# Last three head groups by halves, own buffers for the last batch, and four reorderings, in a fused adaLN attention and adapter block

## The chip, the cores and the metric

One Trainium2 chip, one core, one launch. The metric is the device time of the kernel in microseconds (us). The kernel before took 1140.43 us, the median of three runs (1139.66 to 1143.99).

## The reference

For each of 4 sequences of 1024 tokens and 256 channels (float32): a modulated layer norm, attention with 16 heads of 16 channels, a gated residual, a second modulated norm, and a feed-forward part that picks one of 8 adapters per sequence by the smallest reconstruction loss.

```python
mod = (silu(c) @ wmod).reshape(4, 6, 1, 256)          # sa, ca, ga, sb, cb, gb; |ga|, |gb| at least 0.25
h = layernorm(x) * (1 + ca) + sa
q, k, v = split(h @ qkv_w.T)                          # 16 heads of 16
x = x + ga * (softmax(q @ k.T * 0.25) @ v @ proj_w.T + proj_b)
h = layernorm(x) * (1 + cb) + sb
recon = relu(h @ W_enc[n] + b_enc[n]) @ W_dec[n] + b_dec[n]     # for all 8 n
top = argmin_n mean((recon - h) ** 2)                 # one n per sequence
ad = connected_idx[top]
out = x + gb * (h @ W_base + b_base + relu(h @ W_down[ad] + b_down[ad]) @ W_up[ad] + b_up[ad])
```

## The kernel before

**Steps.** The heads go in groups of 4, so there are 16 groups (b, g), four for each batch b. The scores of a group are made transposed, keys on the partitions, for one half h of the queries (512) and one tile of 128 keys at a time. That is a step: `begin` twice (four matmuls each into `pt`, L707, then an exponential on ACT, L715, into `es`) and `weigh` once (eight matmuls `pv`, L664). A half (b, g, h) has 8 steps, so the list `order` of 32 halves has 256 steps, and the main loop takes two steps at a time (an iteration, k0 = 0, 2, 4 ...). In the order before, both halves of a group stand next to each other, except at the end, where the first halves of groups (3,2) and (3,3) come before their second ones.

**Row maxima.** The exponent needs the maximum of each query's row before the step. `row_max` makes the scores a second time, queries on the partitions, in 32 "pairs" for each group (16 for each half): two matmuls `ps` (L604) and a max on DVE (L611). After the 16 pairs of a half, `to_row` is put in the list `urgent`: a transpose `pmx` on PE (L564), copies on DVE and POOL (L566 to L570), then `store`, which writes the maxima to DRAM (L573), and `back`, which reads them as rows into the tile `mt` (two transfers, L584). The second matmul pair of each `pt` (`pt<-mt,pick`) subtracts them, so the first step of a half needs `mt`. How many pairs stand done at step k is said by `wanted(k)`, a straight line between the points of the list `ends`.

**The planner.** `defer(n, f)` runs f at the n-th `tick` from now; there is one tick at the start of each step. Everything else is in streams: lists of items that wait for a step ("at"), for so many steps ("wait"), or for a condition ("need"), and then emit moves ("X"), dense matmul tiles ("D") or decode tiles ("R"). An iteration has a fixed pattern of tiles, score pairs and weighings (`PATTERN`). At its first V an urgent `to_row` is taken if there is one; otherwise one D, if the streams are pressed, that is if the sum of their paces is over 1.2. At its end it takes one D if one was ready at its top. Up to two R go in an iteration. A stream with a due step (`by`) gets a pace and a rate from what is left; R is taken twice in an iteration only if some stream's rate is over 1. PE and SP run in exactly the order in which they are emitted; the other engines are reordered from step 16 on.

**q and k.** `expand` brings a group's q and k back from DRAM, 256 KB in each of eight transfers (L525), into tiles of three buffers; `fetches` does so from step n * 16 + 1 on for the group n + 2, once the q and k of its channel half are stored.

**After attention.** `post(b)` projects the attention's output of a half (`ppj`, L757), adds the residual, norms (bn_stats, POOL's power, transposes `ptn_n`), encodes (`ph`, L793; ACT, L801) and decodes (`pr`, L814; DVE subtracts, L817; ACT squares and sums, L822). When both halves are done, `choose` (L836 to L868) finds the adapter and gathers its weights, `narrow` makes `pmid` (L905), and `final` makes the last product (`pf`, L928 and L939), added on DVE (L948). `post(b)` runs beside the steps of batch b + 1. For the last batch, the streams called `ending` start with group (3,3), but the first item of `main` waits for the end of post(2), since both use the same buffers (x, gates, gated weights, h2T). What is left of `ending` after the steps goes in an order written out by hand in the last lines.

**The divisor.** For the last channel half of the last batch the sums of the exponentials come straight from `ou` to `su` (L683), and `scaled_last(h)` takes the reciprocal (L650) and multiplies (L651), in two pieces of 256 columns one after the other; the projection of that half needs it.

Of the kernel before, what the change touches and what calls it, by code (L numbers as in the profile page):

```python
# [17 lines left out]
P = 128  # L18
HD = 16
HG = 4  # L20
# [6 lines left out]
def tile_adaln_block(  # L27
# [257 lines left out]
    def defer(steps, f):  # L285
        later.append([steps, f])
# [270 lines left out]
    def row_max(b, g):  # L557

        n = (b * NG + g) % 2
        mx = st.tile([P, NH, NH, HG, TH], F32, tag="mx", name=f"mx_{b}_{g}", bufs=2)  # L560

        def to_row(hq):
            pm = msc_tile([P, P], f"pmx_{b}_{g}_{hq}")
            nc.tensor.transpose(pm, mpad[n], ident)  # L564
            mfull = st.tile([HG * NT, P], F32, tag="mfull", name=f"mfull_{b}_{g}", bufs=1)
            nc.vector.tensor_copy(mfull, pm[: HG * NT, :])  # L566
            mrow = st.tile([HG * NT, 2, P], F32R, tag="mrow", name=f"mrow_{b}_{g}", bufs=1)
            eng = nc.vector if alone else nc.gpsimd
            eng.tensor_copy(mrow[:, 0, :], mfull)  # L569
            eng.tensor_tensor(mrow[:, 1, :], mfull, mrow[:, 0, :].bitcast(F32), ALU.subtract)  # L570

            def store():
                nc.sync.dma_start(  # L573
                    mdram[n][hq].rearrange("l r c -> r l c"),
                    mrow[hq * HG * TH : (hq + 1) * HG * TH].bitcast(F32),
                )
                if alone:
                    back()
                else:
                    defer(1, back)  # L580

            def back():
                for a in range(2):
                    nc.sync.dma_start(  # L584
                        mt[n][a * DUO : a * DUO + HG, hq * HALF : (hq + 1) * HALF].bitcast(F32),
                        mdram[n][hq, :, a * HG * TH // 2 : (a + 1) * HG * TH // 2, :].rearrange(
                            "l (i t) c -> l i (t c)", i=HG // 2
                        ),
                    )

            if alone:
                store()
            else:
                defer(1, store)

        for half in range(NH):
            pairs = [(i, half, t, h) for h in range(NH) for i in range(2) for t in range(TH)]
            for i, hq, t, h in pairs:
                q, k = duos["q", b, g, i], duos["k", b, g, i]
                t0 = hq * HALF + t * P  # L600
                ps = big_tile([P, 2, HALF], f"ps_{b}_{g}_{hq}_{t}_{h}_{i}")
                for a in range(2):
                    r = slice(a * DUO, (a + 1) * DUO)
                    nc.tensor.matmul(  # L604
                        ps[:, a, :],
                        q[r, t0 : t0 + P],
                        k[r, h * HALF : (h + 1) * HALF],
                        start=True,
                        stop=True,
                    )  # L610
                nc.vector.tensor_reduce(mx[:, h, hq, i::2, t], ps, AX.X, ALU.max, negate=True)  # L611
                if (i, hq, t, h) == pairs[-1]:
                    rows = mpad[n][:, : HG * NT].rearrange("p (q j t) -> p q j t", q=NH, t=TH)
                    nc.vector.tensor_tensor(rows[:, half], mx[:, 0, half], mx[:, 1, half], ALU.min)
                    defer(1, lambda half=half: urgent.append(("D", 0.0, [lambda: to_row(half)])))
                yield
# [26 lines left out]

    last_su = {}

    def scaled_last(h):
        su, part = last_su[h], aT_of[B - 1, h][:, NC - 1, :]
        for u in range(2):
            cols = slice(u * HALF // 2, (u + 1) * HALF // 2)
            nc.vector.reciprocal(su[:, cols], su[:, cols])  # L650
            nc.vector.tensor_tensor(part[:, cols], part[:, cols], su[:, cols], ALU.mult)  # L651

    def step_of(b, g):
# [6 lines left out]
        def weigh(h, kt, es):  # L660
# [10 lines left out]
            if kt == NT - 1:  # L671
                if (b, h) not in aT_of:
                    aT_of[b, h] = wp.tile([P, NC, HALF], F32, tag="aT", name=f"aT_{b}_{h}", bufs=3)
                ou = wp.tile([P, HALF], F32, tag="ou", name=f"ou_{b}_{g}_{h}", bufs=1)
                nc.scalar.copy(ou, acc[h])
                to = slice(r0, r0 + HG * HD)
                at = aT_of[b, h][to, ch, :]
                if (b, ch) == (B - 1, NC - 1):
                    nc.sync.dma_start(at, ou[0::2, :])
                if (b, ch) == (B - 1, NC - 1):  # L680
                    if h not in last_su:
                        last_su[h] = wp.tile([P, HALF], F32, tag="su", name=f"su_{b}_{ch}_{h}", bufs=1)
                    nc.sync.dma_start(last_su[h][to, :], ou[1::2, :])  # L683
                    if g == NG - 1 and h < NH - 1:
                        defer(2, lambda: scaled_last(h))
                        defer(4, lambda: done.add((b, ch, h)))
                    return
                j0 = (g % GC) * HG

                def keep():  # L690
                    nc.sync.dma_start(at, ou[0::2, :])
                    nc.sync.dma_start(sdram[ch * NH + h][j0 : j0 + HG, :], ou[1::STRIP, :])
                    if g % GC == GC - 1:
                        defer(1, lambda: turned(b, ch, h))
                        defer(8, lambda: done.add((b, ch, h)))

                defer(1, keep)
# [23 lines left out]
    def post(b, last=False):  # L721
# [1 line left out]
        s = {}  # L723

        def load():
            s["x"] = wp.tile([P, NT, D], F32, tag="x", name=f"x_{b}", bufs=1)
            src = x[b].rearrange("(t p) d -> p t d", p=P)
            for h in range(NH):
                nc.sync.dma_start(
                    s["x"][:, h * TH : (h + 1) * TH, :], src[:, h * TH : (h + 1) * TH, :]  # L730
                )
            s["gt"] = wp.tile([P, 2, D], F32, tag="gt", name=f"gt_{b}", bufs=1)

            nc.gpsimd.dma_start(s["gt"], gates[b].partition_broadcast(P))

# [3 lines left out]
        def gate_proj():  # L739

            ga = s["gt"][:, 0, :]
            s["wpg"] = wp.tile([P, NC, D], F32, tag="wg", name=f"wpg_{b}", bufs=1)
            nc.gpsimd.tensor_tensor(s["wpg"], wproj, per_chunk(ga), ALU.mult)
            s["gpb"] = wp.tile([P, D], F32, tag="gxb", name=f"gpb_{b}", bufs=1)
            nc.gpsimd.tensor_tensor(s["gpb"], ga, pb, ALU.mult)

        def biased(u, what):
# [18 lines left out]
                nc.vector.tensor_tensor(xs, s["po"], xs, ALU.add)  # L766

        def alloc():
            s["h2T"] = wp.tile([P, NC, S], F32, tag="h2T", name=f"h2T_{b}", bufs=1)
            s["acc"] = st.tile([P, NE, NC, NH], F32, tag="sq", name=f"acc_{b}", bufs=1)  # L770

        def normed(half):
            return norm_items(
# [188 lines left out]
        def rec(pr, h):  # L962
            return [("R", lambda c=c: decode(pr, c, h)) for c in range(NC)]

        main = [("need", (b - 1, "end")), ("wait", 2), ("X", load), ("X", alloc), ("wait", 1), ("X", gate_proj)]
        main += [("X", lambda u=u: biased(u, "gpb")) for u in range(NT // 2)]
        for h in range(NH):
            main += [("need", (b, ch, h)) for ch in range(NC)]
# [9 lines left out]
        recs.append(("done", (b, "r")))  # L978
        tail = [("need", (b, "r")), ("wait", 3), ("D", 0.1, [choose]), ("X", gate_out)]
        tail += [("X", lambda u=u: biased(u, "gbb")) for u in range(NT // 2)]  # L980
        tail += [("wait", 1), ("D", FULL, [lambda c=c: narrow(c) for c in range(NC)]), ("wait", 1)]
        each = [(u, t) for u in range(NT // 2) for t in range(2)]
        if last:
            first = [v for v in each if early(v[0])]
# [19 lines left out]

    X_AT = {1: (0, 2), 2: (STEPS + 4, STEPS + 10), 3: (3 * STEPS + 8, 3 * STEPS + 14)}

    groups = [(b, g) for b in range(B) for g in range(NG)]

    order = [(b, g, h) for b, g in groups for h in range(NH)]
    order[-3], order[-2] = order[-2], order[-3]  # L1010
    first_step = {}
    for n, (b, g, h) in enumerate(order):
        first_step.setdefault((b, g), n * NT)
# [152 lines left out]

    def all_maxima():
        yield from maxima
        for b, g in groups[1:-2]:
            yield from row_max(b, g)  # L1170
        last = [row_max(*bg) for bg in groups[-2:]]
        for n in range(2 * PAIRS):
            yield next(last[n * NH // PAIRS % 2])

    def wanted(k):

        ends = [(0, FIRST + 3), (NT - LEAD, PAIRS), (len(order) * NT - NT - LEAD, len(groups) * PAIRS)]
        for (k0, n0), (k1, n1) in zip(ends, ends[1:]):
            if k < k1:
                return n0 + (n1 - n0) * (k + 1 - k0) // (k1 - k0)  # L1180
# [4 lines left out]
    def fetches():  # L1185

        moves = []
        for n, (b, g) in enumerate(groups[2:]):
            moves += [("at", n * STEPS + 1)] + [("need", (w, b, g // GC)) for w in "qk"]
            moves += [("X", lambda b=b, g=g, i=i: expand(b, g, i)) for i in range(2)]  # L1190
            if n + 2 >= NV:
                moves += [("need", ("v", b, NT // 2 - 1)), ("X", lambda b=b, g=g: fetch_v(b, g))]
# [88 lines left out]
    for k0 in range(0, len(order) * NT, 2):  # L1281
        b, g, h = order[k0 // NT]
        if k0 == first_step[b, g]:
# [6 lines left out]
                    left = [36, 28, 28, 18, 12, 0] if b < B - 1 else [34, 26, 26, 12, 8, 0]  # L1290
                    streams += [Stream(items, end - n) for items, n in zip(post(b - 1), left)]
            if (b, g) == groups[-1]:
                ending = [Stream(items) for items in post(B - 1, last=True)]
                streams += ending[:-2]
        if k0 == STEPS:
            begin_order.close()
# [99 lines left out]
```

## Time and profile before

| what | value |
|---|---|
| median of three runs | 1140.43 us |
| the profiled execution | 1141.97 us, span 1140.1 us |
| PE busy | 1079.2 us (95%) |
| DVE busy | 797.2 us (70%) |
| ACT busy | 702.6 us (62%) |
| POOL busy | 262.3 us (23%) |
| last weighing ends, span ends | 1073.1 us, 1140.1 us |
| granted clock of PE, mean | 0.984 |

The times below are of the profiled execution, counted from the start of its span. The activations of L715 are 512, two for each step, so counting them dates each step: step 16 begins its first one at 129.7, step 224 at 953.0, step 240 at 1010.4 and step 246 at 1047.0 us. A number in square brackets at the end of a timeline row is the idle time of that engine just before, and what ended it.

### The profile page before, as it was taken

The page shows a single profiled execution, that of the slowest core. Times are in us where ns is not written, and L with a number is a line of the kernel's source. Part 1 is how long each engine was busy: PE and PEld are TensorE (multiplying, and loading weights), DVE is VectorE, ACT ScalarE, POOL GpSimd, SP SyncE. Part 2 cuts the span into 40 slices and gives each one's busy share as a digit, 9 for nine tenths or more (in the row PEclk, how much of TensorE's full clock was granted, in tenths as well). Part 3 has the DMA queues.
Part 4 walks back from the last instruction along what each step waited for, and adds up shares of the span by engine and source line. Part 5 has one row for each costly group of instructions (what it writes and reads, how often), then busy time and mean ns, then how long its engine had stood idle before and what let it go on. Part 6 is the DMA issues. An engine that isn't in the chain of part 4 may idle for free. (4 is left out here: it accounts for less than half of the span.)

```text
span 1140.1 us, 16544 instructions
## 1 busy us (share of the span) xinstructions
PE 1079.2 (95%) x6371; PEld 482.7 (42%) x6371; DVE 797.2 (70%) x958; ACT 702.6 (62%) x953; POOL 262.3 (23%) x309
## 2 busy tenths in 40 slices
PE   8989899999999999999999999999998999999995
PEld 3433334443444444444544443333544334334433
DVE  5687677667767676777678777877688777872373
ACT  3246566666556677776455777776465677754672
POOL 2214234213243121112435100003221000041103
PEclk9899999999999999999999999999999999999997
DMA  6522423232340302123150303021140200002001
GB/s 185 103 66 90 153 78 119 85 118 71 130 153 39 126 16 91 53 78 100 53 183 6 128 7 99 16 83 27 57 142 2 90 8 16 20 23 85 20 0 49
DMA packets 57799, 84.63 MB, mean 74 GB/s; under 512 B 24940, under 2 KB 40324, under 8 KB 55928
## 3 DMA queue, kind: packets, MB, share of 16 engines
q1 hardware_dynamic: 55824, 80.16, 21.9%
q0 software_dynamic: 1088, 2.36, 0.8%
q8 instruction: 50, 0.82, 0.3%
q10 hardware_dynamic: 808, 1.05, 0.3%
q14 instruction: 29, 0.24, 0.1%
HBM read 52.15 MB, written 24.06 MB: 67 GB/s over the span
## 5 line engine op out<-in xcount | busy, mean ns | idle before, releaser
L611 DVE TENSOR_REDUCE mx<-ps 128x2 f32<-128x1024 f32 x512 | 614.5, 1221 | 196.8 <-PE ps L604 191.2
L715 ACT ACTIVATE es<-pt 128x1024 f32<-128x1024 f32 x512 | 509.4, 1021 | 250.0 <-PE pt L707 229.4
L664 PE MATMUL pv<-es,vaug 128*32 128x512 f32 x2048 | 274.8, 607 | 0.5
L604 PE MATMUL ps<-k,q 64*128 64x512 f32 x1024 | 238.9, 458 | 15.9 <-DVE mx L611 11.6
L707 PE MATMUL pt<-q,k 64*128 64x512 f32 x1024 | 231.1, 435 | 11.1 <-DVE mx L611 7.7
L707 PE MATMUL pt<-mt,pick 64*128 64x512 f32 x1024 | 209.9, 393 | 3.7 <-DMA mt<-mdram 3.7
L604 PEld LDWEIGHTS ps<-k,q 64*128 64x128 f32 x1024 | 97.7, 184 | 223.2 <-issue 91.8
L707 PEld LDWEIGHTS pt<-q,k 64*128 64x128 f32 x1024 | 99.9, 185 | 116.0 <-DVE mx L611 87.7
L822 ACT ACTIVATE df<-df,fbias 128x512 f32<-128x512 f32 x128 | 91.1, 713 | 56.2 <-DVE df L817 56.2
L707 PEld LDWEIGHTS pt<-mt,pick 64*128 64x128 f32 x1024 | 100.6, 186 | 16.4 <-DMA mt<-mdram 4.0
L817 DVE TENSOR_TENSOR df<-pr,h2T 128x1024 f32<-128x1024 f32 x64 | 77.4, 1223 | 21.4 <-PE pr L814 14.9
L664 PEld LDWEIGHTS pv<-es,vaug 128*32 128x32 f32 x2048 | 40.6, 108 | 102.0 <-issue 90.4
L569 POOL CAST mrow<-mfull 32x128 fp32r<-32x128 f32 x31 | 8.7, 281 | 278.6 <-DVE mfull L566 270.7
L814 PE MATMUL pr<-he,wdec 64*128 64x512 f32 x256 | 64.6, 601 | 3.3 <-ACT es L715 3.2
L793 PE MATMUL ph<-h2T,wenc 128*128 128x512 f32 x128 | 62.4, 615 | 0.5 <-ACT h2T L350 0.4
L928 PE MATMUL pf<-wbg,h2T 128*128 128x256 f32 x128 | 37.6, 426 | 1.9 <-DVE x L948 1.9
L319 POOL TENSOR_TENSOR rstd_n<-ve_n,neghalf 128x4 f32<-128x4 f32 x16 | 16.5, 1031 | 86.3 <-DVE ve_n L317 83.5
L505 POOL COPY vaug<-vi 128x512 f32<-128x512 f32 x13 | 8.5, 657 | 111.1 <-DMA vi<-vdram 85.7
L793 PEld LDWEIGHTS ph<-h2T,wenc 128*128 128x128 f32 x128 | 22.0, 189 | 28.4 <-issue 25.2
L466 PE MATMUL pvp<-wqkv,hT 128*128 128x256 f32 x128 | 33.0, 404 | 0.0
L814 PEld LDWEIGHTS pr<-he,wdec 64*128 64x128 f32 x256 | 23.1, 185 | 22.3 <-ACT es L715 6.3
L801 ACT ACTIVATE he<-ph,fbias 128x512 f32<-128x512 f32 x32 | 22.0, 686 | 16.7 <-PE ph L793 16.7
(150 smaller groups left out, 786.0 us busy)
## 6 DMA issues: line engine op xcount, KB each, us to landing
q<-qdram SPq DMA_DIRECT2D x56, 256.0 KB
k<-kdram SPq DMA_DIRECT2D x56, 256.0 KB
qdram<-qhl SPq DMA_DIRECT2D x7, 1024.0 KB
kdram<-khl SPq DMA_DIRECT2D x7, 1024.0 KB
xin<-in_L_attn_x_dram SPq DMA_DIRECT2D x16, 256.0 KB
vdram<-vo SPq DMA_DIRECT2D x16, 256.0 KB
aT<-ou SPq DMA_DIRECT2D x32, 128.0 KB
x<-in_L_attn_x_dram SPq DMA_DIRECT2D x8, 512.0 KB
```

Source lines behind the costliest of these rows:

```text
L466: nc.tensor.matmul(pv[:, t, :], hT[:, c, t0 : t0 + P], wqkv[:, c, 2 * D : 3 * D], start=(c == 0), stop=(c == NC - 1),)
L604: nc.tensor.matmul(ps[:, a, :], q[r, t0 : t0 + P], k[r, h * HALF : (h + 1) * HALF], start=True, stop=True,)
L611: nc.vector.tensor_reduce(mx[:, h, hq, i::2, t], ps, AX.X, ALU.max, negate=True)
L664: nc.tensor.matmul(acc[h][j * STRIP : (j + 1) * STRIP, :], va[:, kt, j, :], es[j // 2][:, j % 2, :], start=(kt == 0), stop=(kt == NT - 1),)
L707: nc.tensor.matmul(pt[:, a, :], k[r, kt * P : (kt + 1) * P] if first else picks[i][r, :], q[r, hs] if first else mt[n % 2][r, hs], start=f ...
L715: nc.scalar.activation(e, pt, AF.Exp, scale=SCALE)
L793: nc.tensor.matmul(s["ph"], wenc[:, c, 2 * pr : 2 * pr + 2, :].rearrange("p n h -> p (n h)"), s["h2T"][:, c, hs], start=(c == 0), stop=(c ...
L801: nc.scalar.activation(s["he", pr, h], s["ph"], AF.Relu, bias=benc_of(pr))
L814: nc.tensor.matmul(two[:, i, :], wdec[r, pr, c * P : (c + 1) * P], he[r, :], start=True, stop=True)
L817: nc.vector.tensor_tensor(df, two, h2T[:, c, hs].unsqueeze(1).to_broadcast([P, 2, HALF]), ALU.subtract)
L822: nc.scalar.activation(df[:, i, :], df[:, i, :], AF.Square, bias=bdec_of(e, c), accum_out=s["acc"][:, e, c, h : h + 1],)
L928: nc.tensor.matmul(po[u][:, t, :], s["h2T"][:, c, t0 : t0 + P], s["wbg"][:, c, :], start=(c == 0), stop=False,)
```

## The change

1. **Order.** `LAST = 3`: the last three groups (3,1), (3,2), (3,3) do their three first halves (steps 208 to 231) and then their three second halves (232 to 255). Their maxima are made in the same order, and `mx` has three buffers. All first halves of the last batch are thus weighed at step 231, where it was step 239.
2. **Buffers of the last batch.** Its x, gates, gated projection weights and bias, h2T and `su` have places that other tiles have left by then (hT, xin, qhl, khl). `main` doesn't wait for the end of post(2) any more. `ending` starts at step 224 (first step of (3,3), before 232) and is due at step 248. `acc` has two buffers.
3. **Divisor.** `scaled_last` works in four pieces of 128 columns; for the first half the pieces go at four successive ticks, and the projection may start at the sixth tick instead of the fourth.
4. **Maxima.** The second point of `ends` is (5, 32) where it was (3, 32): the first group's pairs are spread over five steps, and all later ones lie on a line from (5, 32) to (243, 512). For the first group alone (`soon`) store and back go at once, where they were deferred by one tick each.
5. **First expansion.** `fetches` holds the expansion of group 2 to step 15 at the earliest.
6. **Narrow.** Batches 0 to 2 wait two steps, before one, between the gather and `narrow`.

```diff
-        mx = st.tile([P, NH, NH, HG, TH], F32, tag="mx", name=f"mx_{b}_{g}", bufs=2)
+        mx = st.tile([P, NH, NH, HG, TH], F32, tag="mx", name=f"mx_{b}_{g}", bufs=LAST)
+        soon = b + g == 0
...
-                if alone:
+                if soon:
                     back()
                 else:
                     defer(1, back)
...
-            if alone:
+            if soon:
                 store()
             else:
                 defer(1, store)
...
-    def scaled_last(h):
+    def scaled_last(h, us=range(4)):
         su, part = last_su[h], aT_of[B - 1, h][:, NC - 1, :]
-        for u in range(2):
-            cols = slice(u * HALF // 2, (u + 1) * HALF // 2)
+        for u in us:
+            cols = slice(u * HALF // 4, (u + 1) * HALF // 4)
...
-                        defer(2, lambda: scaled_last(h))
-                        defer(4, lambda: done.add((b, ch, h)))
+                        for u in range(4):
+                            defer(2 + u, lambda u=u: scaled_last(h, [u]))
+                        defer(6, lambda: done.add((b, ch, h)))
...
-            s["x"] = wp.tile([P, NT, D], F32, tag="x", name=f"x_{b}", bufs=1)
+            if last:
+                s["x"] = wa.tile([P, NT, D], F32, tag="hT", name=f"x_{b}", bufs=1)
+            else:
+                s["x"] = wp.tile([P, NT, D], F32, tag="x", name=f"x_{b}", bufs=1)
...
-        main = [("need", (b - 1, "end")), ("wait", 2), ("X", load), ("X", alloc), ("wait", 1), ("X", gate_proj)]
+        main = [] if last else [("need", (b - 1, "end")), ("wait", 2)]
+        main += [("X", load), ("X", alloc), ("wait", 1), ("X", gate_proj)]
...
-        tail += [("wait", 1), ("D", FULL, [lambda c=c: narrow(c) for c in range(NC)]), ("wait", 1)]
+        tail += [("wait", 1 if last else 2), ("D", FULL, [lambda c=c: narrow(c) for c in range(NC)]), ("wait", 1)]
...
+    LAST = 3
...
-    order[-3], order[-2] = order[-2], order[-3]
+    order[-NH * LAST :] = [(b, g, h) for h in range(NH) for b, g in groups[-LAST:]]
...
-        for b, g in groups[1:-2]:
+        for b, g in groups[1:-LAST]:
             yield from row_max(b, g)
-        last = [row_max(*bg) for bg in groups[-2:]]
-        for n in range(2 * PAIRS):
-            yield next(last[n * NH // PAIRS % 2])
+        last = [row_max(*bg) for bg in groups[-LAST:]]
+        for n in range(LAST * PAIRS):
+            yield next(last[n * NH // PAIRS % LAST])
...
-        ends = [(0, FIRST + 3), (NT - LEAD, PAIRS), (len(order) * NT - NT - LEAD, len(groups) * PAIRS)]
+        ends = [(0, FIRST + 3), (NT - LEAD + 2, PAIRS), (len(order) * NT - NT - LEAD, len(groups) * PAIRS)]
...
-            moves += [("at", n * STEPS + 1)] + [("need", (w, b, g // GC)) for w in "qk"]
+            moves += [("at", max(n * STEPS + 1, STEPS - 1))] + [("need", (w, b, g // GC)) for w in "qk"]
...
-                ending = [Stream(items) for items in post(B - 1, last=True)]
+                ending = [Stream(items, len(order) * NT - NT) for items in post(B - 1, last=True)]
```

## The prediction

> **What bounds the kernel now.** I read the page first, then the SP queue and PE around step 16, then the windows of the last 36 steps and the timeline of the end. The page:
>
> ```profile
> PE 1079.2 (95%) x6371; PEld 482.7 (42%) x6371; DVE 797.2 (70%) x958; ACT 702.6 (62%) x953; POOL 262.3 (23%) x309
> ```
>
> PE sets the pace. A step without score pairs takes 2.12 us (plain steps begin at 1048.28 and 1050.40), all of it PE work, beside 1.94 us of exponentials on ACT. A dense tile put into such a step adds its whole length: the two iterations with a projection took 6.17 and 6.18 us, the plain ones 4.3. So work moved from the end into the steps is paid there in full, unless something waits there. Two stretches do wait. The first is at step 16, on SP and then on PE:
>
> ```profile
> 118.84 0.32 SPq L573 DMA_DIRECT2D mdram<-mrow  x1
> 119.26 1.16 SPq L525 DMA_DIRECT2D q<-qdram  x2
> 120.47 1.22 SPq L525 DMA_DIRECT2D k<-kdram  x2
> 121.74 1.23 SPq L525 DMA_DIRECT2D q<-qdram  x2
> 123.01 1.24 SPq L525 DMA_DIRECT2D k<-kdram  x2
> 124.30 1.31 SPq L584 DMA_DIRECT2D mt<-mdram  x2
> ```
> ```profile
> 124.42 0.50 PE L707 MATMUL pt<-q,k 64*128 64x512 f32 x2
> 128.59 0.97 PE L707 MATMUL pt<-mt,pick 64*128 64x512 f32 x2 [3.66 <-DMA mt<-mdram]
> ```
>
> The eight expansions of group 2 (2 MB) are issued between `store` and `back` of group 1's first half. `mt` lands 4.2 us after its issue, behind them, and PE stands for 3.66 us. The second stretch is where post(2) ends (windows by stage: span, then busy time of PE, PEld, DVE, ACT, POOL):
>
> ```profile
> 1010.40:1047.00 36.60, 33.47 (x169) 16.25 (x169) 16.63 (x24) 13.26 (x15) 15.70 (x17) 0.91 0.16 46
> 1047.00:1073.00 26.00, 26.00 (x178) 10.84 (x176) 5.10 (x16) 19.75 (x21) 6.21 (x6) 1.00 0.19 61
> 1073.00:1140.10 67.10, 51.66 (x188) 26.16 (x186) 34.77 (x58) 32.62 (x78) 12.39 (x11) 0.91 0.08 25
> ```
>
> Steps 240 to 245 took 36.6 us. Their PE work by the rows is 6 x 2.12 for the steps, 6 pairs x 0.33, `pmid` 1.94, four finals x 3.4 and 0.3 for `pmx`: 30.5 us. So 6.1 us went into waits there. The steps after that have no gap. The end:
>
> ```profile
> 1074.25 0.60 SPq L683 DMA_DIRECT2D su<-ou  x1
> 1078.42 3.37 DVE L650 RECIPROCAL su<-su 128x256 f32<-128x256 f32 x2 [6.73 <-DMA su<-ou]
> 1084.38 3.72 PE L757 MATMUL ppj<-wpg,aT 128*128 128x256 f32 x16
> 1093.79 3.70 PE L793 MATMUL ph<-h2T,wenc 128*128 128x512 f32 x8 [0.43 <-ACT h2T L350]
> 1117.61 0.64 PE L836 MATMUL pl<-acc,mean_w 128*128 128x32 f32 x2 [5.49 <-ACT df L822]
> ```
>
> The second half of the last batch is a chain: its sums, their reciprocal, projection, norm, encoding, decoding, choice. The first half's encoding and decoding mostly fill the time in which this chain keeps PE waiting.
>
> **The change part by part.**
>
> *First pairs (part 4).* `wanted` gave 8 and 7 pairs in the first two iterations, which took 11.75 and 10.04 us with DVE as the limit (19.5 of 21.8 us busy); the change gives 5 and 5, then 5 where 4 stood (8.12 us). Five pairs fewer at DVE's 1.16 us, one more at 0.4: -5.4, of which I count 5.0. At step 15 four pairs are owed (54 done, not 58). They return at 0.33 us (PE alone) to 1.16 us (DVE): 1.3 to 4.6, I take 2, as most iterations are bound by PE. Sum -3.0.
>
> *Step 16 (parts 4, 5).* The old line is 32 + 2(k - 2), the new one 32 + 480(k - 4)/238. The 48th pair, the last of group 1's first half, moves from iteration 10 to iteration 12, so `to_row` from the first V of iteration 12 to that of 14, `store` to tick 15, `back` to tick 16, the very step that needs it. The hold to step 15 puts the expansions at the end of iteration 14: after `store`, still before `back`. On the old clock `pmx` comes at 121.7, the store at 124.5 (2.8 us for the copies), eight issues of 5.0 us, `back` at 129.9, landing 4.2 us later at 134.1. PE needs it at 124.8. It stands 9.3 us instead of 3.7: +5.6. Bounds: +3.7 (copies at the 1.6 us of an undisturbed half) and +8 (a longer cold phase). What follows the wait costs too: the clock was granted at 0.61 and 0.54 in the two 2 us windows from 128 on, and matmuls there took about twice as long, some 1.8 us. I count that once, as before. The Trainium skill ("TensorE: Matmul & The Clock Gate", What's actually happening) has the clock halved after an idle window of about 3.4 us and restored after about as long a busy one, so the price wouldn't grow with the length of the gap; it would also leave gaps below that unpunished, but here the clock fell to 0.62 and 0.50 after gaps of 1.2 us (at 1011) and 1.9 us (at 1026). By the rule the small waits below cost their length alone, by these rows up to 1.4 us more each.
>
> *Steps 24 to 120 (part 4).* By the same line, each half that begins there gets its `to_row` one iteration later; the line has caught up from step 128 on. So `pmx` to first need shrinks from 4 steps to 2. The chain costs: from `pmx` to the second `mt` issue 3.7 us in undisturbed halves (205.88 to 209.68), and the landing 1.6 us (store to back) to 2.7 us (the least that stood open without a wait, before step 144): 5.3 to 6.4, I take 5.6. Left over is, counting `pmx` 1.6 us after the iteration's first exponential: 5.1 to 5.2 us before steps 8, 32, 40, 72 and 80, 3.3 before step 48, where the iteration was a short one (5.45 us), and 6 or more before the others. Waits of 2.3 + 5 x 0.45 = 4.5, of which I take 4. Bounds: 2 (landing 1.6) and 12 (landing 2.7, and cold phases). Nothing else is queued on SP behind these but x and v, which are early.
>
> *The last groups (parts 1, 2).* The first halves are all weighed at step 231. Pieces of the divisor at ticks 234 to 237, projection allowed at 238. post(2): with the due step 248 `ending` has a rate over 1, so its six last decodes go two to an iteration (224, 226, 228), and `choose` comes at step 232, not 238. `narrow` falls to the end of iteration 236, as its two waits miss 234 and `to_row` takes the V of 236. Then one D at each V and each end: finals at 238, 239, 240, the two projections at 241 and 243, a final at 242. Norm 244 to 247, transposes at 248, encodings at 250, 251, 252, 253, and decodes two in iteration 252 and two in 254. So 1.4 (transposes) + 4 x 1.75 (ph) + 4 x 0.93 (pr) = 12.1 us of PE work come from the end into steps with no gap: +12.1. Bounds: +8 (some encodings miss) and +14.
>
> *Waits around step 240 (parts 2, 3, 6).* Of the 6.1 us there I count half as saved: the reciprocals (1.7 us each, DVE tied up from 1020 to 1028 while PE waited 1.91 us for a final to leave its bank) go into pieces before the finals, and `pmid` comes later after its gather. Bounds 0 and -6. Part 6 for batches 0 and 1 and `acc`: 0, since `pmid` shows no idle time before it there.
>
> *The end.* `su` lands as before, 5.4 us after the last weighing. Four decodes left over (3.7 us of PE) run in that time. Reciprocals 4.3 us in four pieces, half of them before the first projection tile: projection ends about 13.4 us after the last weighing (15.1 before), encoding starts 5.7 us later, at 19.1 (20.8). No old decodes are in the way now, so all four encodings go first (7.0), then decode, subtract (2.5), and ACT's 8 x 1.42 us: 40.0 where `pl` stood at 44.4. From there 22.5 us as before: -4. Bounds -2 and -6.
>
> *Group (3,3)'s expansion* (step 209, first pair end of 211): issued from 885.3 on, needed at 895; no wait, bound 2 us.
>
> Sum: -3.0 + 5.6 + 4 + 12.1 - 3 - 4 = +11.7 us. The profiled execution had 1141.97, 1.5 above the median, so in the median's terms 1152.
>
> **The rivals.**
>
> *A, `mt` in time (not slower).* Place: steps 8 to 120. If the expansions don't stand before `back`, or land early, the wait of 3.66 us and its cold clock (1.8) go and no small waits come: the early parts give -3 - 5.5 = -8.5 instead of +6.6, with +5.1 at the end -3.4: 1137. For it: SP waits for nothing but POOL's copies there, so anything that keeps PE longer in steps 14 and 15 buys lead. Against: the emission order above. It decides when `mt` for step 16 is issued before 124 us of the old clock.
>
> *B, the steps have room.* The 12.1 us go into the 10.9 us that steps 224 to 255 cost above their PE rows (120.0 against 109.1), +1; end -6, waits -0: -5 there, +6.6 early: 1142. Against: the plain iterations of 4.25 us are all PE.
>
> *C, both A and B:* -8.5 - 5 = 1127.
>
> *D, waits compound.* Where POOL or SP was busy the chain took 9.4 to 11.1 us (before steps 8, 16, 32, 80); if four halves meet that with 5 us left, +16 more: 1168.
>
> *E, the first half isn't reached:* the norm ends too late, only 1.4 us move; +6.6 + 1.4 - 3 - 1: 1144.
>
> **How the numbers follow.** Forecast 0.50, A 0.12, B 0.12, C 0.13, D 0.07, E 0.06. A measurement of this kernel tells a change from none at about 0.5%, 5.7 us. Faster: C and a third of A, 0.17. Same: the rest of A, most of B and E and a little of the forecast, 0.24. Slower 0.59. The forecast's own range from the bounds taken together is 1143 to 1163. To hold 8 in 10 the whole range reaches down past A to 1133 and up to 1163.
>
> **What would show it.** Right: `mt` for step 16 issued after the expansions and PE idle for 8 to 10 us there; idle time of `pt<-mt,pick` (3.7 us in all before) at 12 to 18 us; the first two iterations under 17.5 us together; about 12 us more of ph, pr and transposes before the last weighing, which ends 12 to 18 us later; 61 to 65 us from there to the end. Wrong: no longer idle time at step 16 (A), or a last weighing hardly later although ph and pr stand before it (B).

## The result and the profile after

The changed kernel takes 1188.85 us (median of 4 runs, 1186.8 to 1189.5) where the kernel before takes 1141.6 (4 runs on the same chip): a ratio of 1.041, 95% interval 1.0384 to 1.0436. That is 47 us slower. The forecast was 1152 with a range of 1133 to 1163: the direction was right, the size was not. The profiled execution had 1189.01 us, span 1187.2.

The page of the changed kernel, against PE's 1079.2 us (95%) before:

```profile
PE 1096.2 (92%) x6371; PEld 488.5 (41%) x6371; DVE 798.5 (67%) x966; ACT 704.2 (59%) x953; POOL 262.5 (22%) x309
```

PE ran the same 6371 matmuls and was busy 17 us longer, so matmuls became slower; and it stood idle 30 us longer. Dating the steps by the exponentials on ACT says where. All times are us of the profiled executions; "last" is the end of the last weighing.

| stretch | before | after | difference |
|---|---|---|---|
| start to step 8 | 98.9 | 97.0 | -1.9 |
| step 8 to 128 | 474.6 | 509.8 | +35.2 |
| step 128 to 208 | 308.0 | 308.9 | +0.9 |
| step 208 to last | 191.6 | 209.2 | +17.6 |
| last to the end | 67.0 | 62.3 | -4.7 |

The same stretch of steps 8 to 128 by windows, first of before, then of after (span, then busy time of PE, PEld, DVE, ACT, POOL; then granted clock, DMA share, GB/s):

```profile
98.90:573.50 474.60, 460.43 (x2853) 207.73 (x2850) 336.27 (x380) 305.90 (x378) 129.31 (x145) 1.00 0.27 91
```
```profile
97.00:606.80 509.80, 476.07 (x2857) 213.10 (x2854) 339.76 (x382) 306.66 (x378) 131.19 (x147) 0.97 0.26 86
```

The 35.2 us are 15.6 us of longer matmuls (476.07 - 460.43; the mean clock fell to 0.97) and 19.5 us of idle PE. The waits of after in that stretch (total, times, longest):

```profile
PE pt L713 <- DMA mt<-mdram: 18.2, 11, 7.2
PE pt L713 <- DVE mx L614: 7.3, 4, 5.6
```

Before they were 3.7 and 2.7. The 7.2 is step 16, on SP and on PE as predicted:

```profile
120.95 0.32 SPq L576 DMA_DIRECT2D mdram<-mrow  x1
121.36 1.15 SPq L525 DMA_DIRECT2D q<-qdram  x2
122.57 1.22 SPq L525 DMA_DIRECT2D k<-kdram  x2
123.84 1.24 SPq L525 DMA_DIRECT2D q<-qdram  x2
...
126.39 1.31 SPq L587 DMA_DIRECT2D mt<-mdram  x2
```
```profile
130.18 0.97 PE L713 MATMUL pt<-mt,pick 64*128 64x512 f32 x2 [7.15 <-DMA mt<-mdram]
...
256.11 0.87 PE L713 MATMUL pt<-mt,pick 64*128 64x512 f32 x2 [2.49 <-DMA mt<-mdram]
...
310.28 0.80 PE L713 MATMUL pt<-q,k 64*128 64x512 f32 x2 [5.63 <-DVE mx L614]
...
327.23 0.68 PE L713 MATMUL pt<-mt,pick 64*128 64x512 f32 x2 [1.65 <-DMA mt<-mdram]
...
361.84 1.13 PE L713 MATMUL pt<-mt,pick 64*128 64x512 f32 x2 [2.00 <-DMA mt<-mdram]
```

`store` goes out, the eight expansions follow, and `mt` is issued behind them. The other rows are steps 48, 60, 64 and 72. Step 60 is the one that the prediction has nothing on (the expectations below call it step 62). DVE stood there for an x tile:

```profile
308.68 0.43 DVE L312 BATCH_NORM_STATS2 bs_n<-xin 128x6 f32<-128x256 f32 x1 [7.01 <-DMA xin<-in_L_attn_x_dram]
```

By the steps DVE comes to this tile an iteration earlier than before (1.0 us before step 60 begins, where it was 1.0 us before step 62). SP, which issues in the order of emission, couldn't follow: the load at 304.82 stood behind the store of a split q, for which SP had waited 7.6 us until POOL was done, and behind the round trip of the sums, 3.2 us more. On DVE the row maxima `mx` stood behind bn_stats, and PE waited for them.

The clock behind a wait, by windows of 2 us after the 2.49 us at step 48:

```profile
254.00:256.00 2.00, 0.00 (x0) 0.00 (x0) 0.50 (x1) 0.13 (x1) 0.00 (x0) 1.00 0.68 270
256.00:258.00 2.00, 1.89 (x12) 1.02 (x16) 0.75 (x1) 0.93 (x2) 0.00 (x0) 1.00 0.00 0
258.00:260.00 2.00, 2.00 (x12) 0.77 (x6) 0.50 (x2) 1.60 (x3) 0.00 (x0) 0.50 0.00 0
```

Here the clock falls to one half some 2 us after the wait ended, when PE is busy again. Added up over windows of 2 us between steps 8 and 128, the clock took 15.2 us in after (1 less the granted share, times 2 us, for the windows below 0.97) and 1.7 in before. It did so in six places: steps 16 (5 us), 48, 60, 64, 72 and 119. Counted only while PE was busy, the slow phases took 12.2 us in after and 1.6 in before, so they make some 10.5 of the 15.6 us. Much of the rest stands in the two matmuls that first read a late `mt`: 0.68 to 1.13 us at steps 48, 64 and 72 in the rows above, at full clock, against 0.40 for two that did not wait (at 356.85).

The tail, in the rows that answer to those of before (SP, then DVE, then PE):

```profile
1126.07 0.60 SPq L688 DMA_DIRECT2D su<-ou  x1
```
```profile
1128.95 1.76 DVE L653 RECIPROCAL su<-su 128x128 f32<-128x128 f32 x2 [0.58 <-DMA su<-ou]
```
```profile
1130.91 4.97 PE L774 MATMUL ppj<-wpg,aT 128*128 128x256 f32 x14 [3.47 <-DVE aT L654]
...
1141.74 8.96 PE L813 MATMUL ph<-h2T,wenc 128*128 128x512 f32 x16
...
1164.57 0.63 PE L856 MATMUL pl<-acc,mean_w 128*128 128x32 f32 x2 [5.77 <-ACT df L842]
```

`pl` stands 39.7 us after the last weighing (44.5 before), as the sum had it (40.0).

### The profile page after: what moved, and what is told of

Same layout as the page of the kernel before. It is cut to its first block, busy times and chain, and to the rows that moved or that the text cites. A ratio compares the mean times of both kernels' runs of the same rounds, so it can differ in the third digit from the quotient of the medians.

```text
span 1187.2 us, 16522 instructions
## 1 busy us (share of the span) xinstructions
PE 1096.2 (92%) x6371; PEld 488.5 (41%) x6371; DVE 798.5 (67%) x966; ACT 704.2 (59%) x953; POOL 262.5 (22%) x309
## 5 line engine op out<-in xcount | busy, mean ns | idle before, releaser
L667 PE MATMUL pv<-es,vaug 128*32 128x512 f32 x2048 | 277.8, 613 | 1.8 <-ACT es L721 1.4
L607 PE MATMUL ps<-k,q 64*128 64x512 f32 x1024 | 244.4, 461 | 15.4 <-DVE mx L614 8.7
L713 PE MATMUL pt<-q,k 64*128 64x512 f32 x1024 | 235.3, 439 | 20.5 <-DVE mx L614 14.0
L713 PE MATMUL pt<-mt,pick 64*128 64x512 f32 x1024 | 218.4, 396 | 18.5 <-DMA mt<-mdram 18.4
L607 PEld LDWEIGHTS ps<-k,q 64*128 64x128 f32 x1024 | 100.3, 186 | 216.5 <-issue 96.3
L713 PEld LDWEIGHTS pt<-q,k 64*128 64x128 f32 x1024 | 102.6, 186 | 132.7 <-DVE mx L614 93.1
L713 PEld LDWEIGHTS pt<-mt,pick 64*128 64x128 f32 x1024 | 105.2, 187 | 36.6 <-DMA mt<-mdram 23.8
L774 PE MATMUL ppj<-wpg,aT 128*128 128x256 f32 x128 | 33.6, 408 | 3.5 <-DVE aT L654 3.5
L645 POOL TENSOR_TENSOR aT<-aT,su 128x512 f32<-128x512 f32 x14 | 17.9, 1281 | 78.7 <-DMA su<-rdram 75.9
L432 PE MATMUL pq<-hT,wqkv 128*128 128x512 f32 x64 | 33.1, 642 | 1.5 <-DVE loss L860 1.5
```

What stands on the lines that cost most here:

```text
L432: nc.tensor.matmul(pq, wqkv[:, c, n * D + ch * P : n * D + (ch + 1) * P], hT[:, c, hs], start=(c == 0), stop=(c == NC - 1),)
L607: nc.tensor.matmul(ps[:, a, :], q[r, t0 : t0 + P], k[r, h * HALF : (h + 1) * HALF], start=True, stop=True,)
L667: nc.tensor.matmul(acc[h][j * STRIP : (j + 1) * STRIP, :], va[:, kt, j, :], es[j // 2][:, j % 2, :], start=(kt == 0), stop=(kt == NT - 1),)
L713: nc.tensor.matmul(pt[:, a, :], k[r, kt * P : (kt + 1) * P] if first else picks[i][r, :], q[r, hs] if first else mt[n % 2][r, hs], start=f ...
L774: nc.tensor.matmul(s["po"][:, t, :], aT_of[b, t0 // HALF][:, c, t0 % HALF : t0 % HALF + P], s["wpg"][:, c, :], start=(c == 0), stop=(c == ...
```

## The experiments

Theory 1: the pace line through (5, 32) makes 15 halves of the maxima late, and the waits for `mt`, what stands behind them on SP and DVE, and the slower clock after them are the early loss. Theory 2 puts it down to the hold of the expansions, theory 3 to the order and the buffers. For the end: moved PE work paid in full (E1), the order of batch 2's tail (E2), or paired decodings that overload ACT (E3).

**e1: the pace line undone.**

```diff
-        ends = [(0, FIRST + 3), (NT - LEAD + 2, PAIRS), ...]
+        ends = [(0, FIRST + 3), (NT - LEAD, PAIRS), ...]
```

> The changed kernel with one line undone: the second point of the line that paces the score pairs goes back from 4 steps to 2 steps ahead (NT - LEAD); the hold of the first expansions, the changed order and all buffers stay. Theory 1 (late maxima: each half's maxima are begun one iteration later in steps 8 to 120, and the waits for mt, what is queued on SP behind them, and the slower clock after each wait make the 33 us by which the changed kernel lags at step 128): the lag at step 128 falls to 0 or below (the hold now takes the wait of 3.66 us at step 16 away too), and the time is about 1152, that is the 1189 of the changed kernel less 33 to 40 us. Theory 2 (the hold of the expansions to step 15 makes the lag): 1180 to 1189. Theory 3 (order and buffers make it, through other places in memory and other waits): 1180 to 1189 as well.

Measured: 1150.68 us, ratio to before 1.0094 (1.0074 to 1.0115). Steps 8 to 128 take 468.7 us, 41 less than in after:

```profile
100.40:569.10 468.70, 459.16 (x2853) 206.77 (x2850) 336.94 (x380) 305.74 (x378) 132.04 (x148) 1.00 0.28 93
```

PE is busy 17 us less than in after for the same work, at a clock of 1.00. No wait for `mt` is left in that stretch, not even the one of 3.66 us that the kernel before has. With the line undone, `back` is emitted ahead of the held expansions:

```profile
120.33 0.33 SPq L576 DMA_DIRECT2D mdram<-mrow  x1
121.77 1.30 SPq L587 DMA_DIRECT2D mt<-mdram  x2
123.12 1.15 SPq L525 DMA_DIRECT2D q<-qdram  x2
```

**e2: the pace line alone, in the kernel before** (the same line, the other way round).

> The kernel before with that one line of the pace alone (two steps later for the second point). Theory 1: slower by 25 to 38 us, about 1172, the lag at step 128 about 33 us, idle time of PE ahead of pt<-mt,pick 15 us or more. Theory 2 and theory 3: within 4 us of the kernel before, 1138 to 1145, since neither the hold nor the order is there. My prediction's own sum for this edit was -3 + 4 to 6 + 4, that is 1147 to 1149.

Measured: 1169.66 us, 1.0245 (1.0204 to 1.0286), +29 us. Steps 8 to 128 take 505.4 us:

```profile
101.50:606.90 505.40, 478.10 (x2857) 213.43 (x2854) 339.55 (x382) 306.94 (x379) 128.71 (x144) 0.97 0.26 85
```
```profile
PE pt L707 <- DMA mt<-mdram: 11.9, 10, 2.5
PE pt L707 <- DVE mx L611: 7.0, 4, 5.4
```

One line, without order, buffers or hold, brings the stall of 5.4 us at step 60 and the low clock. Of its +30.8 us in this stretch 17.7 are longer matmuls and 13.1 idle time. The idle time for `mt` (11.9 us) is below the 15 us that I expected, the loss is not. Theories 2 and 3 fall for the early part.

**e11: the pace line's point one step later instead of two.**

```diff
+        ends = [(0, FIRST + 3), (NT - LEAD + 1, PAIRS), ...]
```

> The kernel before with the pace line's second point one step later instead of two. By the line's integer arithmetic no half of the maxima then ends in a later iteration than before (all 31 halves six steps ahead of their use), while with two steps 15 of them end four steps ahead; the first two iterations get 6 and 7 pairs instead of 8 and 7. Theory 1 (the late halves make the loss): no loss, the two pairs fewer at DVE's 1.16 us give up to 2.3 us, 1137 to 1140. Rival (fewer pairs at the start have to be made up later, and that costs in proportion): about half of the loss of the two-step edit, 1150 to 1157.

Measured: 1142.59 us, 1.0014 (1.0000 to 1.0027). The loss is not proportional to the shift. By the arithmetic of `wanted`, one step moves no half's last pair into a later iteration and two steps move it in 15 halves. The gain at the start that theory 1 allowed for did not come either: step 8 begins at 99.3, before at 98.9.

**e3: the hold undone in the changed kernel.**

```diff
-            moves += [("at", max(n * STEPS + 1, STEPS - 1))] + ...
+            moves += [("at", n * STEPS + 1)] + ...
```

> The changed kernel with the hold of the first expansions undone (emitted from step 1 on, as before). Theory 1: the wait for mt at step 16 gets smaller by up to 5 us, the rest of the lag stays: 1183 to 1188. Theory 2: the lag goes: about 1155. Theory 3: no change, 1189.

Measured: 1183.31 us, 1.0399 (1.0362 to 1.0435), 5.5 us less than the changed kernel by the medians, though the two intervals overlap. The profiles show the place: PE's wait before step 16 is 1.82 us instead of 7.15, and steps 12 to 20 take 29.3 us instead of 36.3. With the late line and no hold, SP issues the expansions from 106.94 on, ahead of the store at 121.15, and nothing stands between `store` and `back`. Theory 2's 1155 is far off.

**e5: the loads of x earlier in the changed kernel.**

```diff
-    X_AT = {..., 3: (3 * STEPS + 8, 3 * STEPS + 14)}
+    X_AT = {..., 3: (3 * STEPS + 4, 3 * STEPS + 10)}
```

> The changed kernel with the loads of batch 3's x tiles 4 steps earlier (first at steps 52 and 58 instead of 56 and 62), so that they no longer stand on SP behind the later round trips of mt. Theory Q (the queue: DVE waited 7.01 us for such a tile at step 62, and PE 5.63 us for DVE): the steps 60 to 64 fall from 25.4 us to 16 to 18, and the time to about 1181. Rival (the maxima are late by themselves; another wait takes that place): the steps 60 to 64 stay over 22 us or the next ones get longer, 1186 to 1190.

Measured: 1194.51 us, 1.0475 (1.0443 to 1.0507), slower still. Steps 60 to 64 fell from 25.4 us to 20.0, not to 16 to 18. DVE's longest wait for x shrank from 7.01 to 2.4 us, so the queue was what held that load. But the wait moved:

```profile
PE pt L713 <- DMA mt<-mdram: 11.1, 3, 4.8
```

That is the wait for `mt` from step 50 to 72, 3.6 us in after. POOL shows why:

```profile
285.58 3.64 POOL L324 TENSOR_SCALAR xh_n<-xin,mv_n,rstd_n 128x256 f32<-128x256 f32 x3
289.17 0.28 POOL L572 CAST mrow<-mfull 32x128 fp32r<-32x128 f32 x1
...
290.64 0.45 POOL L573 TENSOR_TENSOR mrow<-mfull,mrow 32x128 fp32r<-32x128 f32 x1
```

With x there early, the norm's 3.64 us stand ahead of the maxima's copies, `store` goes 6.8 us after `pmx` (1.6 in after), and `mt` is late at step 56. The rival was nearer, and even its 1186 to 1190 was too low: with the late line, the norm's work on POOL became a wait on PE.

**e7: the hold alone, in the kernel before.**

```diff
-            moves += [("at", n * STEPS + 1)] + ...
+            moves += [("at", max(n * STEPS + 1, STEPS - 2))] + ...
```

> The kernel before with one edit alone: the expansions of groups 2 and later are held to step 14 at least, so that the eight of group 2 are issued behind the second half of the round trip of mt for step 16 instead of ahead of it. Theory 1 (mt for step 16 lands late only because 2 MB of expansions stand ahead of it on SP): the wait of 3.66 us and the slower clock behind it (1.8 us) go, 1134 to 1137, and the steps 12 to 20 take 5 us less. Rival (PE then waits for the next thing, the pairs or group 2's tiles): 1139 to 1143.

Measured: 1135.57 us (11 runs; 1140.12 before), 0.9952 (0.9935 to 0.9968). Steps 12 to 20 take 27.1 us instead of 31.8. The wait of 3.66 us and its cold clock were worth 4.7 us, and nothing took their place.

**e4: the end alone** (pace, hold and `soon` undone, parts 1, 2, 3 and 6 kept).

```diff
-                if soon:
+                if alone:
...
-        ends = [(0, FIRST + 3), (NT - LEAD + 2, PAIRS), ...]
+        ends = [(0, FIRST + 3), (NT - LEAD, PAIRS), ...]
...
-            moves += [("at", max(n * STEPS + 1, STEPS - 1))] + ...
+            moves += [("at", n * STEPS + 1)] + ...
```

> The changed kernel with pace, hold and the immediate store undone: what is left is the order of the last three groups, the last batch's own buffers, the divisor in four pieces and the wait ahead of narrow. Theory 1: no lag to step 208 (within 2 us), then the 17.6 us that the changed kernel lost from step 208 to the last weighing less the 4.7 us that its tail gave back: +13, 1154. Theory 3 (order and buffers make the early lag): 1185 or more. By my prediction's sum for this part (+12.1 - 3 - 4) 1147.

Measured: 1158.43 us, 1.0154 (1.0131 to 1.0176). Steps 8 to 128 take 474.6 us, to the tenth what they took before, so parts 1 to 3 and 6 cost nothing there. From step 208 to the last weighing it takes 208.9 us and from there 62.4, as in after. What it has over the expected 1154 is mostly the start: step 8 begins at 101.8, 2.9 us later than before. But so it does in e7, whose edit acts only later (101.7), while e9 and e10, with e4's code at the start, begin step 8 at 98.9 and 100.1: the start differs that much between profiles of the same code.

**e6 and e9: e4 without the last batch's encodings in the steps, and e4 without the due step.** The edits are, one in each:

```diff
-                streams += ending[:-2]
+                streams += ending[:3]
```
```diff
-                ending = [Stream(items, len(order) * NT - NT) for items in post(B - 1, last=True)]
+                ending = [Stream(items) for items in post(B - 1, last=True)]
```

> The kernel with order, buffers, divisor pieces and narrow's wait alone (1158.4), and in it the last batch's encodings and decodings kept for the time after the last step (only its projection and norm run beside the steps). Theory E1 (the work of 14 us moved into the steps is paid there in full, with waits for ACT beside it): the last weighing comes 14 to 20 us earlier, the tail gets 5 to 12 us longer, 1145 to 1152. Rival E2 (the order, and what it does to batch 2's tail, makes the loss; the moved work only fills gaps): the last weighing comes less than 6 us earlier, 1158 to 1165.

> The kernel with order, buffers, divisor pieces and narrow's wait alone (1158.4), and in it the last batch's streams without the due step 248, so that no iteration takes two decodings. Theory E3 (two decodings in an iteration overload ACT: PE waited for es ahead of pr, pv and pt in 5 to 6 us of such iterations): steps 224 to 256 get 4 to 8 us shorter, 1151 to 1154. Rival E1 (the sum of the moved PE work counts, however it is spread): within 3 us of 1158.4, or longer where what is not reached moves to the tail.

Measured: 1143.59 (1.0020, interval 1.0004 to 1.0036) and 1145.63 (1.0032, 1.0014 to 1.0051), 15 and 13 us under e4 and below every range given. They do not tell E1 from E3, because the two schedules came out nearly the same: in both, batch 2's `choose` goes back to step 238 and the norm's transposes to 251, and at most one encoding fits before the end. Hence the next one.

**e10: the due step and the paired decodings stay, the last batch's encodings go after the steps.**

```diff
-                streams += ending[:-2]
+                streams += ending[:3] + [ending[4]]
```

> The kernel with order, buffers, divisor pieces and narrow's wait alone (1158.4), in which the due step still makes batch 2's last decodings go two to an iteration and its tail come early, but the last batch's four encodings and six decodings stay for the time after the last step. Theory E1 (moved PE work is paid in the steps, about 12.6 us of encodings and decodings after step 248, and the tail gives back little): the last weighing comes 11 to 14 us earlier, the tail gets 3 to 6 us longer, 1148 to 1151; steps 224 to 240 stay at 74 us. Theory E3 (the paired decodings themselves, through ACT, make the loss): 1155 to 1159, since they are still there.

Measured: 1143.31 us, 1.0023 (1.0012 to 1.0034). Windows from step 248 to the last weighing and from there to the end, first of e4, then of e10:

```profile
1059.60:1094.70 35.10, 32.26 (x174) 10.79 (x170) 7.35 (x6) 27.25 (x45) 0.00 (x0) 1.00 0.02 8
1094.70:1157.10 62.40, 42.36 (x138) 22.80 (x138) 27.75 (x56) 19.89 (x48) 11.09 (x10) 0.83 0.08 27
```
```profile
1059.00:1077.00 18.00, 17.99 (x133) 6.45 (x130) 0.00 (x0) 15.89 (x18) 0.00 (x0) 1.00 0.04 15
1077.00:1142.30 65.30, 49.66 (x178) 24.98 (x178) 34.63 (x62) 31.09 (x76) 11.10 (x10) 0.93 0.08 26
```

Four encodings and six and a half decodings cost 17.1 us in the steps: 14.3 of PE work and 2.8 of waits, as an iteration with two decodings also carries their squares on ACT and subtractions on DVE. Taken back to the tail they cost 2.9 us. The paired decodings of batch 2 are still there, and steps 224 to 240 still take 75.8 us (57.4 before, 74.1 after); but steps 240 to 248 give 13 us of that back (27.8 instead of 40.9), since batch 2's tail only moved forward. E1 holds, E3 falls, and even E1's 1148 to 1151 was too high, since the last weighing came 17.8 us earlier and not 11 to 14. Not all of the loss is gone: e10 takes 193.0 us from step 208 to the last weighing, where e2, e7, e11 and e12, with the order of before, take 187.2 to 187.6. Taken without its slow phases of the clock this stretch is 191.3 us in e10, and 190.1 and 191.4 in e6 and e9, which have no paired decodings, so little of the rest is theirs.

**e12: hold and a one-step shift of the pace line, in the kernel before.** e7 and e11 together.

> The kernel before with the hold of group 2's expansions to step 14 and the pace line's second point one step later. Theory 1: both gains add, 1135.6 less up to 2.3: 1133 to 1135. Rival (DVE has nothing to gain at the start, as the slower clock there sets the time): 1135 to 1137.

Measured: 1134.50 us, 0.9950 (0.9933 to 0.9967), inside theory 1's range but not to be told from e7's value. The hold makes the gain.

**e13: the changed kernel with two lines mended** (the pace point at NT - LEAD + 1, the streams without the due step).

> The changed kernel with two lines mended: the pace line's second point one step later than before instead of two, and no due step for the last batch's streams; hold, order, own buffers, divisor pieces stay. Theory (the two lines make the whole loss, the rest is near nothing): 1145.6 less 5 for the wait at step 16 and up to 2.3 at the start, 1138 to 1141. Rival (something else in the order still costs): 1144 or more.

Measured: 1139.66 us, 0.9994 (0.9981 to 1.0008): without the late point and the due step nothing is lost against the kernel before. The rest isn't free, though, and the hold's gain covers it: e13 has e12's pace and a hold one step later, but takes 5.2 us more, and the stretch from step 208 to the last weighing takes 194.6 us (187.5 in e12), of which 5.4 are PE work (185.57 against 180.17: four more encoding matmuls, seven more transposes, and slow phases of the clock in that execution, 3.3 us), and the tail gives back 1.4 us. Whether the order or the buffers make this rest was not tried. So e7 or e12 is the version to keep, some 0.5% under the kernel before.

## Why the prediction was wrong

**Steps 24 to 120, the step that failed.** I took +4 us (bounds 2 and 12). Of the 35.2 us that after lost from step 8 to 128, steps 8 to 24, with step 16 in them, have 5.7 (64.9 us against 59.2) and steps 24 to 128 have 29.5 (444.9 against 415.4). e2, the line alone, measured +29 for the whole kernel. Which halves are late and by how much was right: two steps of lead less in 15 halves. Three things in the price were not:

- *The waits.* 11.0 us in ten places, not 4. The chain from `pmx` to the store took 3.5 us before step 32, where POOL was busy with a norm and a split k, and 4.0 us before step 72, where POOL first multiplied the attention's output by a divisor that had just landed; I had used the undisturbed 1.6. (The two times that I gave for `pmx` and the second `mt` issue are 3.8 us apart and not 3.7, which changes little.) Rival D names this, but with a chance of 0.07, and its 1168 is still 21 us short.
- *What is queued behind.* "Nothing else is queued on SP behind these but x and v, which are early": this was wrong, x was not early any more. DVE stood 7.01 us for it, and PE 5.63 for DVE.
- *The clock.* The prediction read off the rows of before that a short gap costs up to 1.4 us more in slower matmuls, and then left this out of the sum; only the upper bound of 12 names it. Apart from step 16 the clock took 10.2 us in after (15.2 less 5.0), in five places, some 2 us each.

The Trainium skill ("TensorE: Matmul & The Clock Gate", What's actually happening) has the clock halved after an idle window of about 3.4 us, in a window that runs freely. The free window agrees with the traces, where the clock goes to 0.50 and back only at moments whole multiples of 3.41 us apart (last section). The threshold does not: PE waits of 2.49, 2.00 and even 1.56 us (e2, step 16) were enough here. A wait of 2.39 us before step 32 left the clock at 1.00 in after, while one of 2.40 us in e2 brought it to 0.50.

**Step 16** was right: the expansions stand ahead of `back`, and PE waits 7.15 us (forecast 9.3 with copies of 2.8 us; they took 1.6, the lower bound, which gave 7.4). Steps 12 to 20 took 36.3 us against 31.8, +4.5 for the +5.6. It takes both edits: with the late line alone (e2) they took 32.1, with the hold alone (e7) 27.1.

**First pairs**: the first two iterations took 18.0 us (forecast under 17.5, before 21.8), but by step 8 only 1.9 us were left, and e11 and e12 show no measurable gain from fewer first pairs. The -3 is not confirmed; it lies inside the spread of the start between profiles.

**Moved work**: forecast +12.1 for four encodings, four decodings and the transposes, and measured 17.1 for four and six and a half with the waits they bring (e10). The transposes came at step 245 and the encodings at 248 to 251, three and two steps before the forecast, so more decodings went ahead of the end. Rival B, that the steps have room for it, is refuted: the 18.0 us without it are all PE.

**Waits around step 240**: forecast -3, measured none. 4.3 of the 6.1 us that I had found there were no fixed cost of the schedule. Steps 240 to 244 by windows, before and then e7, which runs the same 124 matmuls there:

```profile
1010.40:1039.30 28.90, 25.77 (x124) 12.37 (x124) 15.65 (x22) 9.36 (x11) 13.85 (x14) 0.88 0.17 48
```
```profile
1007.40:1032.00 24.60, 22.71 (x124) 11.22 (x124) 15.05 (x22) 9.18 (x11) 14.05 (x14) 1.00 0.18 57
```

In that one execution a wait of 1.9 us met a fall of the clock; in e7 that wait was 0.5 us and the clock stayed at 1.00. A single profile can't say which of its cold phases come back.

**The end**: -4 forecast, -4.7 measured, inside 61 to 65 us. Together the end was +12.9 instead of +5.1. The profile of before has those slow phases in it: against e2, e7, e11 and e12, which run the same code there in 255.8 to 256.5 us, the 271.5 us of after are some 15 more.

## What to carry to other kernels

A small transfer that an in-order engine waits for needs a lead that covers the slowest case of its whole chain, each queue included; below that, each late arrival holds what stands behind it on the queues and makes waits in places that have nothing to do with it. Price a short wait on a saturated TensorE at its length plus the slow phase that may follow (here 3.41 us at half clock, or a multiple), and try whether the loss has a threshold: here one step of shift was free and two cost 29 us. Before work is moved out of a tail into a loop, look at what it costs where it is: work that fills the gaps of a chain is nearly free there (2.9 us for 14.3 us of TensorE time), and full price where TensorE has no gap.

## What the runs showed of the hardware

Work taken out of the tail made the rest of the tail slower. Without the encodings and decodings e4's tail has 40 matmuls fewer than e10's (138 against 178), but PE is busy only 7.3 us less (42.36 against 49.66), while the same work was 14.3 us in the steps; the granted clock of that stretch falls from 0.93 to 0.83. Counted while PE was busy, the slow phases took 7.4 us there and 1.6 in e10, which is most of the difference. That the gaps lower the clock there is read off the traces and was not tried by itself.

The clock follows a fixed grid, and not the single wait. In each of the 14 profiles the clock changes only at moments whole multiples of 3.41 us apart, so a slow phase lasts 3.41 us or a multiple of it. What goes with a fall is the time that PE idles between two such moments. Counted over all profiles from the first step on, a stretch at full clock with less than 1.1 us of idle PE was never followed by 0.50 (0 of 4179), one with more than 1.75 us always was (59 of 59), and in between it was in 26 of 103. Idle times are rough here, as the ends of matmuls are modelled. This fits the pair of equal waits before step 32. In after the moment 193.12 cuts the wait of 2.39 us (from 191.98 to 194.37) in two, 1.14 and 1.26 us of idle PE, and the clock stays:

```profile
189.71:193.12 3.41, 2.27 (x10) 1.46 (x10) 1.62 (x2) 1.40 (x2) 0.02 (x1) 1.00 0.67 274
193.12:196.54 3.42, 2.16 (x16) 1.01 (x16) 0.92 (x1) 1.08 (x2) 0.00 (x0) 1.00 0.32 120
196.54:199.95 3.41, 3.41 (x30) 1.32 (x22) 2.02 (x3) 2.36 (x3) 0.00 (x0) 1.00 0.11 41
```

In e2 one stretch has 1.90 us of the 2.40, and the clock falls at its end, half a microsecond before the wait is over (194.78):

```profile
190.88:194.29 3.41, 1.51 (x7) 0.78 (x6) 0.86 (x1) 0.64 (x2) 0.00 (x0) 1.00 0.78 315
194.29:197.70 3.41, 2.92 (x12) 1.65 (x16) 1.18 (x1) 1.29 (x2) 0.00 (x0) 0.50 0.21 79
```

So the fall can also come late: after the wait that ended at 256.11 the clock stayed at 1.00 until 257.98.
